# New order lists for every engine: GpSimd's wide sums laid away from VectorE's two-operand work in SBUF

## The chip, the cores and the metric

The kernel runs on one core of one Trainium2 chip. A core has five engines that run side by side, each through its own list of instructions in order: TensorE (PE in the profile, with its weight loads as PEld), VectorE (DVE), ScalarE (ACT), GpSimd (POOL) and SyncE (SP), which here only issues DMAs. They meet through semaphores: an instruction waits at the head of its engine's list until what it needs is there, and everything behind it on that engine waits with it. The metric is the time of one execution on the device, in microseconds; the runs of the kernel before took 1015.21 to 1023.01, with a median of 1018.05 over three.

## The reference, cut to what matters

There are 16 x 512 = 8192 tokens `x` of 512 float32 numbers. For every token the reference computes

```python
h = _ln(x, pw_g[pathway_ids], pw_b[pathway_ids])            # _ln: mean and variance over the 512
h = _ln(h, cp_g[compartment_ids], cp_b[compartment_ids])
t = _ln(x, tm_g[time_steps], tm_b[time_steps])              # time_steps == compartment_ids here
m, n, r = [x + _mlp_ln(state, ...)[:, None, :] for each of three conditions of the batch]
s = _ln(x, ms_g[scale_type], ms_b[scale_type])
w = softmax(aw)
cat = concatenate([w[0]*h, w[1]*t, w[2]*m, w[3]*n, w[4]*r, w[5]*s])      # 6 * 512 wide
out = x + _ln(silu(cat @ int_W1 + int_b1) @ int_W2 + int_b2, int_g, int_be)
```

There are 500 pathways, 5 compartments (and time steps) and 3 scale types by the table sizes. Everything is float32.

## The kernel before, in words

**What is multiplied.** The wide product `cat @ int_W1` is split into three products of 512 x 512 for each token: block X is `x` itself against the weighted sum of the three blocks for `m`, `n`, `r`; block H is the doubly normalised `h` against the first block; block V is the normalised `x` against one matrix that holds both `t` and `s`, `vs`, made from two blocks of `int_W1` with the gammas of the token's compartment and scale as row factors. What depends on the batch and the tables alone is a row that is gathered and added (`ga`). To have one such matrix for a whole tile, the kernel first sorts the tokens by compartment and scale (that is most of the head).

**Groups and tiles.** The sorted tokens are worked on in 16 groups ("windows") of 512, each of four tiles of 128 tokens. `build` (L337, L339 to L342; step `bd`) and `s_part` (L325, `sp`) make a new matrix where a group starts a new one. Where two tiles share a matrix and for X and H always, the 2 x 2 blocks of tokens and features are multiplied by a scheme with seven half-sized products in place of eight: `half_product` (L553, `m7`), `norm_product` (L565, `v7`), `seventh` (L672, `q7`, the second layer). Such a scheme needs sums and differences of the operands and of the results. Those of the operands are made on VectorE (`token_sum`, L508 to L516, `u1` to `u4`; `norm_sum`, L527 to L533, `yv`) or on GpSimd (`z_sums`, L658 to L664, `zs`: 128 x 256 in SBUF); those of the results on VectorE from PSUM (`half_out` L589 to L595, `r2`, `r3`, `r5`; `hidden_add` L598, `ha`; `sum_first` L689 and L691, `sf`; `sum_last` L700 and L702, `sl`) and on ScalarE (`copy_first` L580, `cf`; `keep_first`, `keep_last` L682 to L695, `kf`, `ku`). GpSimd's other wide sum is `shift_x` (L468, `sh`): it adds the last bias row to a tile of `x`, 128 x 512 in SBUF, four in each group.

**The way of a group.** GpSimd gathers the four tiles of `x` (`gx`), the rows of the pathway tables (`gh`, into two buffers), of the compartments (`gc`, two buffers) and the added rows (`ga`, four buffers), all L229. ScalarE takes the sums for mean and variance (`xs`, `fs`, L427 to L429); VectorE and GpSimd make the root of the variance (`xe`, `xp`; `fv` L445, `fp` L449); VectorE multiplies (`front_1`, L423 and L424, `f1`; `front_less`, L460, `f2`); ScalarE scales (`nv` L394, `fn` L453). VectorE then turns each tile in blocks of 32 x 32 (L255: `tx`, `tv`, `th`, `tz` for X, V, H and the hidden layer Z) into a tile `rX`, `rV`, `rH` or `rZ`, and SyncE spreads it by four DMAs of 64 KB for each quarter (`spread_row`, L263, `sX`, `sV`, `sH`, `sZ`) into `catX` to `catZ`, from which TensorE multiplies. The hidden layer goes through `ha`, a silu (`hs`, L601), `tz`, `sZ` and `q7`; then `lq` (L738), `lv` (L746) and `lp` (L751) give the last variance, `lb` (L759 and L760) normalises and adds `x`, and `po` (L764) puts the rows out by a DMA with indices, from GpSimd.

**What sets the order.** Nothing reorders: `tc.manual_schedule()` leaves each engine's instructions as the program emits them, and the program emits them by three lists of step names. `ORDER` is the head with the first two groups; `WINDOW` is run for group numbers 2 to 11, and its names hold a letter for the group (`o`, `p`, `c`, `n`, `m`: two before, one before, this, the next, the one after), so that the work on neighbouring groups interleaves; `LAST` names the rest. A name that has been run is passed over:

```python
for w in range(2, 12):
    run(WINDOW, w)
run(LAST)
```

Each engine's list is thus the subsequence of steps that it has a part in. Several tiles share a buffer and so order the work as well: `rV` and the operand sums of V (`sv`, written by `yv`) lie in one buffer, likewise `rH` with `ss` and `rZ` with `zs`; `x` has three buffers for the groups in flight, so a gather `gx` waits for the `lb` of the group three before.

Of the kernel before, what the change touches and what calls it, by code (L numbers as in the profile page):

```python
# [1716 lines left out]
```

## Time and profile before

| | before |
|---|---|
| median of three runs | 1018.05 us (1015.21 to 1023.01) |
| the profiled execution | 1015.54 us, its span 1013.5 us |
| granted TensorE clock, mean | 0.964 |
| busy share of TensorE, VectorE, ScalarE, GpSimd | 89%, 87%, 57%, 67% |

One execution of the program was taken by the profiler. A row of the timeline or of the groups gives the line of the program, the engine, the operation, what it writes and reads (out<-in), the shape, and how often; busy time is in microseconds, the mean of one instruction in nanoseconds. Idle time in front of an instruction is put down to what ended it. "Issue" is time in which the engine waited for nothing that the profile shows. The last `lv` steps (L746) of consecutive groups serve as marks for the length of a group: they start at 191.2 and at 738.3 us with ten groups between them. Ends of matmuls are modelled, and spans on GpSimd are rough.

### The profile page before, as it was taken

To read this page: it belongs to the slowest core of one execution; us is meant where nothing else is said; L and a number is where in the kernel's file an instruction comes from. 1 tells how busy PE (TensorE), PEld (TensorE's weight loads), DVE (VectorE), ACT (ScalarE), POOL (GpSimd) and SP (SyncE) were. 2 spreads that over 40 slices of the span, in tenths; PEclk is the share of its full clock that TensorE was granted. 3 is DMA by queue.
4 is the path that set the end of the run, shared out by engine and by line. 5 is a ranking of instruction groups with operands and counts; after the bars stand their busy time and mean duration, and the time that the engine had idled before them with its cause. 6 is when DMAs were issued, how large, how long until landed. Compare 5 with 4: busy or idle time off the path is not lost.

```text
span 1013.5 us, 14659 instructions
## 1 busy us (share of the span) xinstructions
PE 904.0 (89%) x3908; PEld 702.9 (69%) x3909; DVE 882.7 (87%) x1476; ACT 573.6 (57%) x1357; POOL 675.5 (67%) x735
## 2 busy tenths in 40 slices
...
GB/s 295 204 137 199 199 248 157 131 191 149 232 186 214 191 172 199 184 209 181 172 190 217 180 236 167 193 196 207 191 230 168 77 204 178 195 169 168 133 50 117
DMA packets 88513, 185.45 MB, mean 183 GB/s; under 512 B 24324, under 2 KB 24324, under 8 KB 88428
## 3 DMA queue, kind: packets, MB, share of 16 engines
...
HBM read 100.48 MB, written 19.97 MB: 119 GB/s over the span
## 4 chain that ended last, share of the span: by engine, by line
DVE 29%; PE 21%; issue 11%; SPq 8%; ACT 7%; DMA 4%; another core or an unknown queue 2%; POOL 1%; ACTq 0%; DVEq 0%; POOLq 0%
SPq L263 8%; PE u L553 6%; PE p L572 4%; PE p L553 3%; DMA catX<-rX 3%; DVE rV L255 3%; PE u L565 2%; PE pq_0b L672 2%; DVE pw L460 2%; DVE pw L423 2%; DVE sv L531 2%; DVE rX L255 2%; DVE vs L337 2%; ACT junk L738 2%
## 5 line engine op out<-in xcount | busy, mean ns | idle before, releaser
L764 POOL DMA_INDIRECT out<-yb,tok x64 | 69.7, 1089 | 67.0 <-issue 28.8
L553 PE MATMUL p<-wh__81,catH 128*128 128x256 f32 x480 | 111.4, 379 | 0.0
L553 PEld LDWEIGHTS p<-wh__81,catH 128*128 128x128 f32 x480 | 91.1, 190 | 13.0 <-issue 0.7
L229 POOL DMA_INDIRECT xbs<-in_x,tok x64 | 63.4, 990 | 48.5 <-DVE yb L760 27.6
L427 ACT ACTIVATE junk<-xbs 128x512 bf16<-128x512 f32 x64 | 40.1, 626 | 97.2 <-DMA xbs<-in_x,tok 73.4
L229 POOL DMA_INDIRECT pw<-in_pw,i_pw x64 | 64.1, 1001 | 33.7 <-issue 15.7
L229 POOL DMA_INDIRECT add<-rows,i_add x64 | 68.0, 1063 | 26.1 <-issue 12.8
L449 POOL TENSOR_TENSOR rsh<-veh,mhalf 128x1 f32<-128x1 f32 x64 | 48.2, 756 | 53.9 <-DVE veh L445 53.3
L468 POOL TENSOR_TENSOR xbs<-xbs,rows 128x512 f32<-128x512 f32 x64 | 83.5, 1309 | 0.5
L553 PE MATMUL u<-wt,catX 128*128 128x256 f32 x240 | 64.4, 417 | 21.3 <-ACT p L580 20.3
L229 POOL DMA_INDIRECT cp<-cp_rows,i_cp x64 | 67.7, 1058 | 23.1 <-issue 14.0
L601 ACT ACTIVATE add<-add 128x512 f32<-128x512 f32 x64 | 38.7, 626 | 76.6 <-DVE add L598 42.6
L565 PE MATMUL u<-vs,sv 128*128 128x256 f32 x276 | 70.1, 384 | 7.7 <-DVE sv L531 3.7
L553 PEld LDWEIGHTS u<-wt,catX 128*128 128x128 f32 x240 | 48.6, 207 | 34.3 <-ACT p L580 25.1
L424 DVE SCALAR_TENSOR_TENSOR pw<-pw,rsx 128x512 f32<-128x512 f32 x64 | 64.5, 1007 | 3.2 <-POOL rsx L377 0.9
L598 DVE TENSOR_TENSOR add<-p,add 128x512 f32<-128x512 f32 x64 | 42.2, 665 | 26.7 <-remote 19.8
L394 ACT ACTIVATE xm<-xbs,nmx,rsx 128x512 f32<-128x512 f32 x64 | 49.4, 805 | 28.1 <-DVE nmx L388 18.9
L337 DVE SCALAR_TENSOR_TENSOR vs<-wt,sct,vs 128x512 f32<-128x512 f32 x72 | 64.7, 957 | 0.4 <-ACT vs L325 0.4
L565 PEld LDWEIGHTS u<-vs,sv 128*128 128x128 f32 x276 | 50.9, 190 | 20.0 <-DVE sv L531 5.1
L427 ACT ACTIVATE junk<-pw 128x512 bf16<-128x512 f32 x60 | 37.7, 629 | 47.7 <-DVE pw L424 16.8
L453 ACT ACTIVATE pw<-pw,rsh 128x512 f32<-128x512 f32 x64 | 44.5, 714 | 34.5 <-POOL rsh L449 15.4
L759 DVE SCALAR_TENSOR_TENSOR yb<-yb,rsy,rows 128x512 f32<-128x512 f32 x60 | 57.5, 959 | 1.6 <-POOL rsy L751 1.6
...
## 6 DMA issues: line engine op xcount, KB each, us to landing
...
```

Of the source, the lines that this page charges most:

```text
L229: nc.gpsimd.indirect_dma_start(dst, None, table, bass.IndirectOffsetOnAxis(ap=idx, axis=0), **kw)
L255: nc.vector.transpose(rot[:, :, :, j, :].rearrange("p q c t -> p c q t"), src.rearrange("p (c q t) -> p c q t", c=NC, q=Q))
L263: nc.sync.dma_start(st[cat][q * L : (q + 1) * L, g].rearrange("p c t -> p (c t)"), st[rot][g * L : (g + 1) * L, q].rearrange("p c j t -> p ...
L337: nc.vector.scalar_tensor_tensor(v[:, c], wt[:, c], sct[:, c, g, w : w + 1], v[:, c], ALU.mult, ALU.add)
L394: nc.scalar.activation(t, st["xb"][:, j, :], AF.Identity, bias=st["nm"][:, j : j + 1], scale=st["rs"][:, j : j + 1])
L424: nc.vector.scalar_tensor_tensor(h, h, st["rs"][:, j : j + 1], pw[:, D:], ALU.mult, ALU.add)
L427: nc.scalar.activation(junk, x, AF.Identity, accum_out=sums[:, 0, k : k + 1])
L468: nc.gpsimd.tensor_add(st["xb"][:, j, :], st["xb"][:, j, :], rows[:, 2, :])
L553: nc.tensor.matmul(dst, m[:, c], at_["half1"][k][:, c], start=(k in (1, 1 if one_matrix(st, a) else 5) and c == 0), stop=(c == NC - 1), sk ...
L565: nc.tensor.matmul(dst, m[:, c], v_half(k)[:, c], start=(k == 5 and c == 0), stop=(c == 1), skip_group_check=True)
L759: nc.vector.scalar_tensor_tensor(y, y, st["rsy"][:, j : j + 1], rows[:, 1, :], ALU.mult, ALU.mult)
L764: nc.gpsimd.indirect_dma_start(out_rows[j], bass.IndirectOffsetOnAxis(ap=tok[:, j, w : w + 1], axis=0), yb[:, j, :], None)
```

## The change

The three lists are replaced. The steps are the same ones, with the same instructions and operands; `ORDER` holds the same 545 names, and a few names move between `WINDOW` and the lists around it because the cut between two groups lies elsewhere (for instance `u1`, `u4`, `m7.0.2` and `m7.0.6` of a group now end its own pass of `WINDOW` instead of beginning the next one). What changes is the order of each engine's instructions in the head, in the repeated groups and in the tail. GpSimd's wide sums, `zs` and `sh`, get other neighbours: in `WINDOW` for instance `sh` of tile 2 moves from the end of its own group, amid `f1`, `sf`, `sl`, to the next group behind `tz.p.1`, and `sh` of tiles 0 and 1 stand among the steps `r3`, `r5`, `ha`, whose second operand is in PSUM. Nothing in the program's functions changes.

The diff, with `WINDOW` whole and the two long lists cut to their ends:

```diff
 ORDER = """
-    lt wk.1.0 sz scl fg h2.2 lo ax g4 dk cv cg xt.0.2 xs.0.0 sp.0.0 se pwi g6 h2.1 gh.0.0 gh.0.2 he.1 fl.2 fl.0 g5 h2.0
-    bx fl.3 wm.4 by xs.0.2 dp xs.0.3 kd gt.0.0 gt.0.2 gt.1.2 gt.0.1 he.2 eh.2 cw gt.0.3 he.0 eh.1 xs.0.1 xt.0.0 xt.0.3
-    pk xe.0 xp.0 xv.0.2 xv.0.0 eh.0 cs tt cp dc gt.1.1 xm.0 nv.0.3 xt.0.1 lh tb vt.0.3 nv.0.1 vt.0.1 tk.0 gx.e0.0 f1.0.2
...
-    gc.2.2 lb.0.3 m7.1.0.5 r5.1.1 kb.1.1 gx.3.0 m7.1.1.2 u4.1.1 m7.1.0.2 u4.1.0 r2.1.0 po.0.2 th.2.1 m7.1.0.4 r2.1.1
-    ha.1.1 sp.2.0 r3.1.1 bd.2.0 th.2.0 r5.1.0 gh.2.2
+    sz h2.0 dk se h2.1 h2.2 g6 xs.0.1 he.1 xs.0.0 he.0 he.2 ax ac eh.1 xt.0.3 g4 xs.0.3 pwi xs.0.2 wk.1.2 xe.0 gh.0.0
+    scl wk.1.0 sp.0.0 g5 dp fg xt.0.0 xv.0.3 bx by kd xp.0 lt tt xm.0 nv.0.3 gh.0.2 xt.0.2 nv.0.0 xv.0.0 eh.2 dc eh.0 cs
+    cv lo fl.3 xv.0.2 gt.0.1 gt.0.2 lw wm.1 lh cg tb wh pk vt.0.3 vv.0.3 fl.2 vt.0.0 cw cp cn gt.0.0 wk.2.2 gt.1.3 ct
...
+    gx.3.0 po.0.0 sh.2.1 m7.1.1.5 m7.1.0.5 fn.2.1 xs.3.2 u4.1.0 r5.1.1 th.2.1 r3.1.1 gh.2.2 r2.1.1 sh.1.1 m7.1.0.4
+    ha.1.1 r2.1.0 po.0.2 fn.2.0 th.2.0 r5.1.0 bd.2.0
 """
...
 WINDOW = """
-    m7.p.0.2 u4.p.0 fp.c.1 fn.c.1 u1.p.1 m7.p.1.2 m7.p.0.6 u4.p.1 m7.p.1.6 lp.o lb.o.3 kb.p.0 r2.p.0 kz.m.2 po.o.3 va.n
-    lb.o.0 gx.n.0 m7.p.1.5 sp.c.0 bd.c.0 m7.p.0.5 sh.p.0 r5.p.1 gc.c.3 lb.o.2 sV.c.3 gx.n.2 xs.n.0 gx.n.3 r3.p.1
-    m7.p.0.3 m7.p.1.4 th.c.1 ha.p.0 r2.p.1 u3.c.0 ha.p.3 hs.p.3 r3.p.0 gh.c.2 th.c.0 m7.p.0.4 ha.p.1 r5.p.0 hs.p.0
-    gh.c.3 hs.p.1 lb.o.1 tz.p.3 po.o.1 m7.c.0.1 v7.c.0.1 m7.p.1.3 tz.p.0 ha.p.2 po.o.2 cf.c.0 m7.c.0.7 v7.c.0.2 hs.p.2
-    sV.c.1 yv.c.0.3 gc.c.2 v7.c.0.7 kb.p.1 xs.n.3 tz.p.1 sh.p.1 sX.c.2 gx.n.1 tz.p.2 m7.c.1.1 ga.c.3 yv.c.0.1 cf.c.1
-    f1.c.2 v7.c.0.5 yv.c.0.2 yv.c.0.4 fs.c.2 f1.c.3 v7.c.0.3 fv.c.2 v7.c.0.6 sX.c.3 u3.c.1 ga.c.1 v7.c.0.4 sp.c.2 bd.c.2
-    v7.c.1.1 sZ.p.0 q7.p.0.1 q7.p.0.2 kz.p.1 fs.c.3 po.o.0 fv.c.3 fp.c.2 cf.c.2 m7.c.1.7 yv.c.1.3 f2.c.2 f2.c.3 sZ.p.1
-    xs.n.1 sh.c.3 fn.c.2 th.c.2 sZ.p.2 fp.c.3 fn.c.3 th.c.3 zs.p.0 tx.n.1 v7.c.1.7 q7.p.0.7 zs.p.1 q7.p.0.5 zs.p.2
-    yv.c.1.1 yv.c.1.2 yv.c.1.4 kf.p.0 cf.c.3 q7.p.0.6 v7.c.1.5 v7.c.1.6 xs.n.2 vd.n gh.n.0 kf.p.1 sf.p.1 zs.p.3 q7.p.0.4
-    sf.p.0 q7.p.0.3 xe.n sZ.p.3 gh.n.1 xp.n tx.n.3 v7.c.1.3 ku.p.0 kb.p.2 sH.c.1 q7.p.1.1 q7.p.1.2 zs.p.4 tx.n.0 zs.p.5
-    sl.p.0 xm.n tx.n.2 sH.c.0 gc.n.1 sl.p.1 nv.n.3 nv.n.1 kb.p.3 q7.p.1.5 kz.p.0 q7.p.1.7 tv.n.3 tv.n.1 sH.c.2 sH.c.3
-    f1.n.0 nv.n.0 gc.n.0 nv.n.2 tv.n.2 kf.p.2 v7.c.1.2 tv.n.0 sV.n.2 kf.p.3 sf.p.3 fs.n.0 zs.p.6 q7.p.1.6 q7.p.1.4
-    ku.p.1 f1.n.1 sf.p.2 fs.n.1 sh.c.2 lq.p.1 sV.n.0 sl.p.2 f2.n.0 zs.p.7 q7.p.1.3 sl.p.3 lq.p.2 kz.c.3 ga.c.2 lq.p.3
-    fv.n.0 ga.c.0 fv.n.1 f2.n.1 u2.c.0 sX.n.1 u2.c.1 lq.p.0 u1.c.0 sX.n.0 lv.p fp.n.0 fn.n.0 v7.c.1.4
+    fp.c.1 fv.c.0 v7.p.1.2 sp.c.0 bd.c.0 r3.p.0 r2.p.0 va.n m7.p.1.2 lb.o.0 gx.n.0 gc.c.2 m7.p.1.6 u4.p.1 lb.o.3 fp.c.0
+    po.o.3 lb.o.2 sX.c.0 m7.p.1.5 r5.p.1 kb.p.1 m7.p.0.4 ha.p.1 sh.p.1 r3.p.1 m7.p.0.5 sV.c.2 fn.c.1 sX.c.2 fn.c.0
+    th.c.1 sV.c.3 u3.c.0 xs.n.0 th.c.0 gx.n.2 gh.c.2 gh.c.3 sh.p.0 r5.p.0 m7.p.1.4 ha.p.3 hs.p.1 m7.p.0.3 ha.p.0 r2.p.1
+    m7.p.1.3 hs.p.3 tz.p.3 ha.p.2 ga.c.3 kb.p.0 hs.p.0 tz.p.0 tz.p.1 m7.c.0.1 sX.c.3 sh.p.2 hs.p.2 tz.p.2 sZ.p.0
+    v7.c.0.1 cf.c.0 gx.n.3 gc.c.3 m7.c.1.1 m7.c.0.7 yv.c.0.1 xs.n.2 yv.c.0.3 v7.c.0.7 cf.c.1 po.o.0 yv.c.0.2 f1.c.2
+    v7.c.0.2 po.o.2 yv.c.0.4 v7.c.0.3 sp.c.2 ga.c.1 lb.o.1 v7.c.0.4 po.o.1 v7.c.0.5 v7.c.0.6 gx.n.1 f1.c.3 u3.c.1 bd.c.2
+    fs.c.2 fv.c.2 fp.c.2 f2.c.2 fs.c.3 kz.o.3 fv.c.3 fp.c.3 yv.c.1.3 v7.c.1.1 cf.c.2 sZ.p.1 zs.p.0 f2.c.3 fn.c.2 th.c.2
+    fn.c.3 q7.p.0.1 zs.p.1 th.c.3 zs.p.2 tx.n.1 m7.c.1.7 v7.c.1.7 kf.p.0 gh.n.0 q7.p.0.7 q7.p.0.5 tx.n.2 xs.n.3 kf.p.1
+    sf.p.1 vd.n zs.p.3 tx.n.3 sh.c.3 q7.p.0.2 xs.n.1 xe.n xp.n q7.p.0.6 gh.n.1 sf.p.0 yv.c.1.1 sZ.p.2 sZ.p.3 zs.p.4
+    zs.p.5 zs.p.6 gc.n.0 sH.c.3 ku.p.0 sl.p.0 yv.c.1.2 cf.c.3 kb.p.2 xm.n yv.c.1.4 nv.n.3 q7.p.0.3 sH.c.1 q7.p.0.4
+    sl.p.1 v7.c.1.5 v7.c.1.6 v7.c.1.3 sH.c.0 q7.p.1.2 tx.n.0 kb.p.3 nv.n.1 tv.n.3 nv.n.0 tv.n.1 q7.p.1.5 q7.p.1.1 kf.p.3
+    f1.n.0 tv.n.0 kz.p.1 q7.p.1.7 sf.p.3 kf.p.2 q7.p.1.6 kz.m.2 sH.c.2 nv.n.2 v7.c.1.4 tv.n.2 ku.p.1 sf.p.2 sl.p.2
+    f1.n.1 u2.c.0 kz.m.0 fs.n.0 u2.c.1 ga.c.2 lq.p.0 zs.p.7 q7.p.1.3 q7.p.1.4 sl.p.3 m7.c.0.2 u1.c.0 sV.n.1 u4.c.0
+    m7.c.0.6 sV.n.0 gc.n.1 fs.n.1 fv.n.1 f2.n.1 u1.c.1 lq.p.1 ga.c.0 lq.p.2 lq.p.3 lv.p lp.p sX.n.1 f2.n.0
 """
 LAST = """
-    lp.10 va.15 gc.12.2 m7.11.1.2 u4.11.1 sV.12.3 u1.11.1 sX.12.2 m7.11.0.2 fp.12.1 fn.12.1 lb.10.1 kb.11.1 gx.13.1
-    m7.11.0.6 r3.11.0 r2.11.0 m7.11.1.6 sh.11.0 r2.11.1 m7.11.1.4 lb.10.2 gx.13.2 sp.12.0 po.10.2 ha.11.3 lb.10.0
...
-    ga.15.3 sh.15.1 u4.15.1 m7.15.1.5 lq.14.0 m7.15.0.5 m7.15.0.6 r2.15.0 r3.15.0 m7.15.1.6 r2.15.1 r3.15.1 kb.14.3
-    r5.15.1 r5.15.0 hs.15.1 m7.15.0.3 m7.15.1.4 sh.15.2 ha.15.0 hs.15.0 m7.15.1.3 ha.15.3 hs.15.3 tz.15.0 q7.14.1.5
-    sh.15.3 q7.14.1.7 w2 tz.15.1 ha.15.2 tz.15.3 hs.15.2 tz.15.2 kf.14.3 sf.14.3 q7.14.1.1 kf.14.2 q7.14.1.6 ku.14.1
-    zs.14.7 q7.14.1.4 q7.14.1.3 sl.14.2 sh.14.0 sl.14.3 q7.14.1.2 lq.14.3 sZ.15.0 sf.14.2 lq.14.2 lv.14 lp.14 lb.14.0
-    po.14.0 lb.14.1 po.14.1 lb.14.3 po.14.3 lb.14.2 l2.15.0 la.15.0 yg.15.0 lq.15.0 sZ.15.1 l2.15.1 po.14.2 la.15.1
-    yg.15.1 lq.15.1 sd.15.1 rv.15.1 ft.15.1 po.15.1 sd.15.0 rv.15.0 sZ.15.2 l2.15.2 la.15.2 yg.15.2 ft.15.0 po.15.0
-    lq.15.2 sZ.15.3 sd.15.2 rv.15.2 ft.15.2 l2.15.3 la.15.3 yg.15.3 lq.15.3 sd.15.3 rv.15.3 po.15.2 ft.15.3 po.15.3
+    va.13 kb.11.0 sV.12.3 kb.11.2 r3.11.0 fp.12.1 fn.12.1 gc.12.3 fv.12.0 fp.12.0 fn.12.0 m7.11.1.6 r2.11.1 sX.12.0
+    r3.11.1 r2.11.0 sX.12.2 lb.10.3 gx.13.3 v7.11.1.2 sV.12.2 xs.13.3 lb.10.2 gx.13.2 m7.11.0.4 m7.11.1.2 xs.13.2
...
+    cf.15.3 bd.15.3 sH.15.2 lW.15.3 m7.15.1.2 ga.15.3 sH.15.3 m7.15.1.4 u2.15.1 u2.15.0 u1.15.0 m7.15.0.5 m7.15.0.6
+    u4.15.0 ku.14.1 sl.14.2 sl.14.3 u4.15.1 u1.15.1 m7.15.1.5 lq.14.1 e1 lq.14.3 lq.14.0 sf.14.2 ga.15.2 lq.14.2 lv.14
+    ga.15.0 m7.15.1.6 r5.15.0 r2.15.0 r3.15.0 lp.14 lb.14.3 po.14.3 ha.15.3 r5.15.1 r3.15.1 hs.15.3 m7.15.0.3 ha.15.0
+    hs.15.0 r2.15.1 tz.15.3 m7.15.1.3 ha.15.2 hs.15.2 tz.15.0 m7.15.0.4 ha.15.1 hs.15.1 sh.14.1 tz.15.2 tz.15.1 sZ.15.0
+    sh.14.2 lb.14.2 lb.14.0 w2 po.14.0 po.14.2 sh.15.1 lb.14.1 po.14.1 sh.15.2 l2.15.0 la.15.0 yg.15.0 lq.15.0 sh.15.3
+    sZ.15.2 l2.15.2 la.15.2 lq.15.2 yg.15.2 sd.15.0 rv.15.0 ft.15.0 po.15.0 sd.15.2 sZ.15.1 l2.15.1 la.15.1 yg.15.1
+    rv.15.2 sZ.15.3 ft.15.2 po.15.2 lq.15.1 sd.15.1 rv.15.1 ft.15.1 l2.15.3 la.15.3 lq.15.3 po.15.1 yg.15.3 sd.15.3
+    rv.15.3 ft.15.3 po.15.3
 """
```

More of the change, by code (lines that the diff above doesn't have):

```diff
@@ new lines @@
+    nv.0.2 nv.0.1 wk.1.3 gc.0.2 xt.0.1 xv.0.1 do va.0 ca gt.0.3 cm cr f1.0.0 gc.0.0 tk.0 wk.1.1 vt.0.1 gx.e0.0 vv.0.0
+    gx.e0.3 vv.0.1 vt.0.2 wk.2.0 gx.e0.2 vv.0.2 f1.0.2 gt.1.1 rp.1 rc.1 ro.1 gx.e0.1 wk.2.1 rp.0 rc.0 wk.2.3 lX.0.0
+    fs.0.0 xs.e0.0 xs.e0.3 gt.1.0 lX.0.1 fs.0.2 f2.0.0 fv.0.0 fp.0.0 fl.0 xs.e0.1 fv.0.2 fp.0.2 f2.0.2 vd.0 bd.0.0
+    gr.e0.0 fn.0.2 ht.0.2 gr.e0.1 xs.e0.2 xe.e0 rp1 gh.0.1 xa.0 xp.e0 xm.e0 ro.0 lX.0.2 fn.0.0 ht.0.0 wm.3 gt.1.2 tk.1
+    gx.e1.0 gx.e1.1 gx.e1.3 xs.e1.1 ea.0 nv.e0.0 gx.1.0 gh.0.3 fl.1 mt.e0.0 nv.e0.1 mt.e0.1 rp2 ar ey.0 ez.0 f1.0.1
@@ L54 @@
+    lq.0.0 lq.0.1 lq.0.3 lq.0.2 lv.0 u1.1.1 sX.2.2 nv.2.0 tv.2.0 r3.1.0 nv.2.2 tv.2.2 sV.2.1 fs.2.0 sV.2.2 fv.2.0 gc.2.2
+    lp.0 sh.1.0 sV.2.3 fp.2.0 lb.0.2 gx.3.2 m7.1.0.2 kb.1.0 lb.0.3 lb.0.0 kb.1.1 sp.2.0 m7.1.1.2 u4.1.1 f2.2.0 sV.2.0
+    gx.3.0 po.0.0 sh.2.1 m7.1.1.5 m7.1.0.5 fn.2.1 xs.3.2 u4.1.0 r5.1.1 th.2.1 r3.1.1 gh.2.2 r2.1.1 sh.1.1 m7.1.0.4
+    ha.1.1 r2.1.0 po.0.2 fn.2.0 th.2.0 r5.1.0 bd.2.0
 """
 WINDOW = """
[L58 removed]
@@ new lines @@
+    q7.11.1.7 sf.11.3 lq.11.0 fs.13.1 fv.13.1 ga.12.0 sV.13.2 q7.11.1.6 ku.11.1 kb.12.0 u2.12.0 u1.12.0 sX.13.0
+    q7.11.1.4 gc.13.0 u2.12.1 fs.13.0 fp.13.1 f2.13.1 fn.13.1 q7.11.1.3 sl.11.2 sl.11.3 m7.12.0.5 lq.11.2 ga.12.3
+    lq.11.3 sp.13.1 fv.13.0 u1.12.1 m7.12.0.2 r5.12.0 sX.13.2 m7.12.0.6 va.14 lv.11 u4.12.1 m7.12.1.5 m7.12.1.6 u4.12.0
+    fp.13.0 f2.13.0 fn.13.0 lp.11 lb.11.3 gx.14.3 lb.11.2 xs.14.3 r3.12.0 th.13.1 r3.12.1 r2.12.0 th.13.0 lb.11.0
+    r2.12.1 m7.12.0.4 ha.12.1 hs.12.1 m7.12.1.3 ha.12.2 r5.12.1 hs.12.2 m7.12.0.3 ha.12.0 hs.12.0 po.11.2 tz.12.2
```

144 lines of the change are left out of this document (66 added, 78 removed).

## The prediction

> **What bounds the kernel now.** I read the page first, for its time and each engine's share.
>
> ```profile
> span 1013.5 us, 14659 instructions
> PE 904.0 (89%) x3908; PEld 702.9 (69%) x3909; DVE 882.7 (87%) x1476; ACT 573.6 (57%) x1357; POOL 675.5 (67%) x735
> ```
>
> Two engines are nearly full: TensorE (PE) and VectorE (DVE). A share over the whole span says nothing of a stage, so the second view is the table of stretches: head, first group, ten groups of the steady loop together, two groups alone, tail, end.
>
> ```profile
> 0.00:130.00 130.00, 108.68 (x568) 64.69 (x569) 88.16 (x220) 76.22 (x192) 95.63 (x167) 0.95 0.64 208
> 130.00:191.20 61.20, 51.29 (x196) 37.45 (x196) 47.13 (x66) 30.67 (x76) 38.15 (x37) 0.94 0.61 176
> 191.20:738.30 547.10, 503.90 (x2240) 424.00 (x2239) 514.60 (x824) 314.67 (x758) 378.75 (x377) 0.98 0.67 193
> 356.30:413.70 57.40, 51.06 (x226) 43.35 (x225) 55.07 (x87) 33.05 (x80) 38.31 (x38) 0.97 0.64 184
> 413.70:467.00 53.30, 49.63 (x225) 42.02 (x225) 50.45 (x79) 30.55 (x75) 38.41 (x38) 1.00 0.68 198
> 738.30:990.80 252.50, 227.77 (x881) 171.59 (x880) 218.58 (x342) 146.78 (x321) 152.77 (x146) 0.95 0.55 156
> 990.80:1013.50 22.70, 12.36 (x29) 5.13 (x27) 14.21 (x25) 5.24 (x13) 10.23 (x9) 0.82 0.36 119
> ```
>
> The columns are length, then busy time (and count) of PE, PEld, DVE, ACT, POOL. The ten steady groups take 547.1 us, 54.7 each. A plain group (413.7 to 467.0) takes 53.3, with PE busy 49.6 and VectorE 50.5. A group that also rebuilds the products' matrix (356.3 to 413.7; eight more VectorE instructions) takes 57.4, with VectorE busy 55.1. So VectorE looks like the fuller engine. But is all of that work? The third view, the timeline, says no:
>
> ```profile
> 452.04 0.71 POOL L658 TENSOR_TENSOR zs<-catZ 128x256 f32<-128x256 f32 x1
> 452.05 0.98 DVE L700 TENSOR_TENSOR yb<-yb 128x256 f32<-128x256 f32 x1
> 456.08 1.24 POOL L662 TENSOR_TENSOR zs<-catZ 128x256 f32<-128x256 f32 x1
> 456.78 2.33 DVE L424 SCALAR_TENSOR_TENSOR pw<-pw,rsx 128x512 f32<-128x512 f32 x1
> 457.30 1.26 POOL L468 TENSOR_TENSOR xbs<-xbs,rows 128x512 f32<-128x512 f32 x1
> 458.52 1.17 POOL L664 TENSOR_TENSOR zs<-catZ,zs 128x256 f32<-128x256 f32 x1
> 459.03 1.29 DVE L255 STREAM_TRANSPOSE rV<-xm 128x512 f32<-128x512 f32 x2
> 461.33 0.75 DVE L424 SCALAR_TENSOR_TENSOR pw<-pw,rsx 128x512 f32<-128x512 f32 x1
> 472.97 2.46 DVE L759 SCALAR_TENSOR_TENSOR yb<-yb,rsy,rows 128x512 f32<-128x512 f32 x1
> 473.58 1.29 POOL L468 TENSOR_TENSOR xbs<-xbs,rows 128x512 f32<-128x512 f32 x1
> 486.57 2.19 DVE L527 TENSOR_TENSOR sv<-catV 128x256 f32<-128x256 f32 x1
> 487.18 1.28 POOL L468 TENSOR_TENSOR xbs<-xbs,rows 128x512 f32<-128x512 f32 x1
> ```
>
> Columns: start, duration. The same L424 takes 0.75 when GpSimd (POOL) does no wide sum and 2.33 beside two of them; two transposes (L255) beside a wide sum keep their 0.65 each. An operation with its second operand in PSUM is not slowed either:
>
> ```profile
> 148.91 1.28 POOL L468 TENSOR_TENSOR xbs<-xbs,rows 128x512 f32<-128x512 f32 x1
> 149.02 0.69 DVE L598 TENSOR_TENSOR add<-p,add 128x512 f32<-128x512 f32 x1 [6.26 <-issue]
> ```
>
> What this costs in a plain group, by the groups of 413.7 to 467.0 against the free durations:
>
> ```profile
> L759 DVE SCALAR_TENSOR_TENSOR yb<-yb,rsy,rows 128x512 f32<-128x512 f32 x4 | 4.7, 1171 | 0.0
> L424 DVE SCALAR_TENSOR_TENSOR pw<-pw,rsx 128x512 f32<-128x512 f32 x4 | 4.6, 1146 | 0.1
> L460 DVE SCALAR_TENSOR_TENSOR pw<-pw,sumsh,cp 128x512 f32<-128x512 f32 x4 | 3.8, 977 | 0.0
> L527 DVE TENSOR_TENSOR sv<-catV 128x256 f32<-128x256 f32 x2 | 3.1, 1536 | 0.0
> L531 DVE TENSOR_TENSOR sv<-catV 128x256 f32<-128x256 f32 x2 | 2.7, 1372 | 0.0
> ```
>
> ```profile
> L531 DVE TENSOR_TENSOR sv<-catV x23: 402/416/3105, 155.5 to 758.7; 128x256 f32<-128x256 f32 x23
> ```
>
> With 0.75 free for the three wide lines and 0.42 (the median above) for the two narrow ones: L759 4.7 − 3.0 = 1.7, L424 4.6 − 3.0 = 1.6, L460 0.8, L527 3.1 − 0.84 = 2.3, L531 1.9. Together 8.3 us. The four `sh` sums (L468) carry most of it, 1.6 to 1.8 each; a `zs` sum costs some 0.5 (L700, 0.98 where 0.42 is free: 0.56). Without them VectorE would do 42 us of work in a group of 53.3, and PE would be the bound.
>
> What PE loses is in the waits of a plain group and of one that rebuilds:
>
> ```profile
> PE pq_1b L672 <- DVE yb L691: 1.2, 1, 1.2
> PE p L565 <- DVE sv L533: 1.0, 1, 1.0
> PE u L565 <- DVE sv L527: 0.5, 1, 0.5
> ```
>
> ```profile
> PE u L553 <- ACT p L580: 4.5, 1, 4.5
> ```
>
> In the plain group 2.7 of its 3.7 us of PE idle time end at a VectorE instruction queued behind one that a wide sum had held. In the rebuilding group 4.5 of 6.3 end at `cf` (L580), the copy that lets a second product be added on.
>
> **The change part by part.** Instructions and data stay; only lists move. The first term is the wide sums' place. I read it from the new WINDOW by what stands before each sum in GpSimd's list, since that is what holds it at run time. `sh.p.1` stands behind `po.o.3`, which waits for `lb.o.3`; the put-out costs about 1 us, in which VectorE does `lb.o.2`; then come `r5`, `ha`, `r3`, all with an operand in PSUM: free. `sh.p.0` stands behind `gh.c.2` (it reuses a buffer that `th.c.0` frees) and `gh.c.3`; after `th.c.0` VectorE has `r5`, `ha`, `ha`, `r2` and transposes: free. `sh.p.2` stands behind `ga.c.3`, whose buffer `tz.p.3` frees; `ha.p.2` and three transposes follow, some 2.7 us by the rows above (0.69 + 3 × 0.65), against 1 us of gather and 1.28 of sum: just free. `sh.c.3` follows `zs.p.3` behind `gh.n.0`, beside transposes and `sf`: free if GpSimd is not late. Of the eight `zs`, numbers 1, 2 and 3 lie beside transposes and `sf`; 0, 4, 5, 6, 7 still meet `f2`, `sl`, `yv` or `u`. In the old list the next two VectorE steps behind each of the four `sh` hold four steps with such an operand pair; in the new one they hold one (the `yv` behind `sh.p.2`). So 3 × 1.75 = 5.2 of 8.3 go: 0.6 of the contention.
>
> What that is worth in time is bounded by PE. Plain groups: six, with at most 53.3 − 49.6 = 3.7 to win; of the 2.7 that waits name I take 0.6, 1.6, rounded to 1.5: 6 × 1.5 = 9. Rebuilding groups: four, the first of the ten among them, which waits alike:
>
> ```profile
> PE u L553 <- ACT p L580: 5.4, 1, 5.4
> ```
>
> The old ACT list has three silus ahead of `cf.c.0`, the new one four, so `cf` now waits for `ha.p.2`. From `bd.c.0` to `ha.p.2` VectorE has 31 instructions in the new list, at about 0.65 some 20 us, and PE has 19 us of products ahead of the one that needs `cf`: ten `m7` (eight `m7.p`, `m7.c.0.1`, `m7.c.1.1`) by 1.73 and two `v7` by half of that. The 1.73 is half the step between two runs of sixteen matmuls, two products each:
>
> ```profile
> 251.58 3.62 PE L553 MATMUL u<-wt,ss 128*128 128x256 f32 x16
> 255.03 3.62 PE L553 MATMUL u<-wx__80,ss 128*128 128x256 f32 x16
> ```
>
> Counted in the same way the old lists have about 20 against 20, and yet PE waited 4.5, because VectorE came into the group late by what contention had cost it in the group before. With 5.2 less it comes in early: of 4.5 I take 3.0, 4 × 3.0 = 12. Below: nothing gained, 0. Above: all PE idle time of the steady stretch, 547.1 − 503.9 = 43.
>
> Head (0 to 191.2): only reordered, with hardly a wide sum before 130. PE idles 21.3 + 9.9 there. Moves in both directions; bounds ±6, value 0. Tail (738.3 to 990.8): by the same reading 16 `sh` meetings become 12, 4 × 1.75 = 7 us of VectorE time, at the steady rate (21 us of time for 52 of contention) 3 us. End (22.7): all `q7` now precede the last `m7`; that uncovers the last `ha`, `tz` and spread (before, seven `q7` of 0.87 lay over them) and takes `lb.14` out of the end: 0, ±4.
>
> Other queues: the gathers `gx`, `gh`, `gc`, `ga` and the put-outs `po` change places on GpSimd, which is busy 38.4 of 53.3; ACT, which waits for their landings, has 30.6 of 53.3. Those slacks hide them; if they fail, ACT's `cf` is late, as now. `kz` does nothing after the first group. The weight loads keep SP's order but for table loads in the head.
>
> Sum: −9 − 12 − 3 = −24. Profiled execution 1015.5 (span 1013.5 and 2.0 around it) becomes 991.5; the median of the runs, 1018.05, lies 2.5 above it, so 994.
>
> [...]
>
> **The rivals.** (1) The sums run away from their places: forecast no change. For it: in the old list `zs.p.6` stands behind `sf.p.3`, and it ran at 456.08, before `f1.n.1`'s L424 at 461.33 by five microseconds, in the midst of the earlier L424. If the new places drift alike, other operand pairs are met, contention stays at 8.3 and the time with it: 1016. Against: three of four `sh` now stand right behind a step that waits for VectorE.
>
> (2) PE becomes the full bound: plain groups fall to about 50.5, rebuilding ones to 52, 547 to 511; −36 there and −4 in the tail: 978. For it: VectorE would have eight microseconds to spare. Against: latencies of the spreads are not shortened.
>
> (3) Slower: the spreads through SP. The first `yv` writes a tile in the buffer that `rV` holds, so it must wait for the last `sV` spread.
>
> ```profile
> 407.09 4.97 SPq L263 DMA_DIRECT2D catV<-rV  x8
> 417.22 6.27 SPq L263 DMA_DIRECT2D catV<-rV  x8
> 431.74 0.41 DVE L531 TENSOR_TENSOR sv<-catV 128x256 f32<-128x256 f32 x1
> ```
>
> A spread is four issues, 4.97 / 2 = 2.5 us. The last `sV` was sixth of a run of eight spreads, issued by 423.5, and the first `yv` ran at 431.7: 8.2 later, of which some 3 are landing. Now the last `sV` is seventh: 2.5 later, and VectorE arrives 5 earlier. Behind `yv` queue `f1`, `bd`, `f2` and all that PE's `v7` needs. It decides from the point where the last `sV` lands over 8 us after VectorE is free for it; if that holds PE 4 us a group, ten groups give +40, less the 24: 1034.
>
> **How the numbers follow.** Forecast 0.50, its own range 983 to 1007; rival 2 0.16; rival 1 0.22; rival 3 0.12. The likeliest is 994. For 8 in 10 the range takes rival 1 whole and most of rival 2: 975 to 1024. About 1% (1008 to 1028) is what a measurement of this kernel can tell from no change. Forecast and rival 2 lie below: faster 0.66; rival 1: same 0.22; rival 3: slower 0.12.
>
> **What would show it.** Right: L527, L531, L424, L759 near their free means in the steady groups, VectorE busy about 45 in a plain one, `pq_1b <- yb L691` and `u <- p L580` smaller, groups of some 52 and 54. Wrong: those groups as long as before with VectorE idle instead (rival 3, with a wait for catV or catX in front of L527 or L531), or the same excess at other lines (rival 1).

## The result and the profile after

Four runs of the changed kernel took 981.35 to 988.67 us, with a median of 983.36; the kernel before took 1015.21 to 1023.01 beside them, with a median of 1017.68. The ratio is 0.966, with a 95% interval of 0.961 to 0.972: 34 us faster, where 24 were forecast. The profiled execution of after is the slowest of its four runs (988.67). The same kernel was therefore profiled once more on another chip (called "after again" here): 979.70 against 1018.42 us, a ratio of 0.963 (0.959 to 0.968), its profiled execution 976.82. Lines in after are one higher than in before, since the lists are one line longer; in the experiments they are up to four higher.

The head of the page of after, and its stretches cut at the same marks as before (the last `lv`, now L747): head, ten steady groups, tail with end, and one plain group. Columns as in the prediction.

```profile
span 986.8 us, 14570 instructions
PE 902.2 (91%) x3908; PEld 707.5 (72%) x3909; DVE 787.2 (80%) x1476; ACT 578.6 (59%) x1357; POOL 670.5 (68%) x735
```

```profile
0.00:190.80 190.80, 162.66 (x752) 103.14 (x754) 125.83 (x283) 105.02 (x261) 133.24 (x201) 0.92 0.63 196
190.80:730.00 539.20, 504.89 (x2251) 430.84 (x2250) 450.77 (x827) 321.69 (x764) 373.06 (x377) 0.98 0.68 196
730.00:986.80 256.80, 234.70 (x908) 173.51 (x906) 210.57 (x368) 151.87 (x335) 164.22 (x157) 0.97 0.57 164
...
514.00:567.50 53.50, 50.54 (x226) 43.50 (x225) 43.00 (x80) 30.93 (x74) 37.12 (x38) 0.97 0.68 197
```

The steady groups and the tail of after again, and one of its plain groups:

```profile
194.80:722.20 527.40, 499.68 (x2252) 427.25 (x2251) 450.94 (x828) 322.16 (x764) 371.71 (x377) 0.99 0.70 201
722.20:975.00 252.80, 233.00 (x908) 172.82 (x906) 208.82 (x367) 151.73 (x334) 164.39 (x157) 0.97 0.58 167
...
409.00:460.40 51.40, 48.83 (x226) 42.33 (x225) 42.98 (x79) 31.04 (x74) 37.12 (x38) 1.00 0.71 205
```

VectorE's work in the steady groups falls from 514.6 to 451 us in both, with the same instructions. What that is worth differs between the two executions: 547.1 us of steady groups become 539.2 in one and 527.4 in the other. The tail with its end was 275.2 (252.5 and 22.7 in the prediction's rows) and is 256.8 and 252.8. The head was 191.2 and is 190.8 and 194.8.

The groups of VectorE's instructions in that plain group of after (514.0 to 567.5), with the lines that the prediction named:

```profile
L425 DVE SCALAR_TENSOR_TENSOR pw<-pw,rsx 128x512 f32<-128x512 f32 x4 | 3.0, 752 | 0.1
L760 DVE SCALAR_TENSOR_TENSOR yb<-yb,rsy,rows 128x512 f32<-128x512 f32 x4 | 3.0, 745 | 0.0
...
L256 DVE STREAM_TRANSPOSE rH<-pw 128x512 f32<-128x512 f32 x4 | 2.7, 701 | 3.9 <-ACT pw L454 3.9
...
L528 DVE TENSOR_TENSOR sv<-catV 128x256 f32<-128x256 f32 x2 | 2.1, 1030 | 0.0
...
L532 DVE TENSOR_TENSOR sv<-catV 128x256 f32<-128x256 f32 x2 | 0.8, 413 | 0.0
```

L425, L760 and L532 are free (they meant 1146, 1171 and 1372 before). L528 is the one pair that the prediction left: one `yv` a group still meets `sh.p.2`. Against the free durations a plain group has 2.2 us of excess over all of VectorE's lines, where the same count gives 9.7 before. So the contention went as planned. The new row is 3.9 us in front of `th` (L256): VectorE now waits for ScalarE, whose own wait stands one step earlier, at the copy `cf.c.2` (below). Where TensorE waits in the steady groups, before, in after and then in after again:

```profile
PE u L553 <- ACT p L580: 15.4, 7, 5.4
PE pq_1b L672 <- DVE yb L691: 12.1, 10, 1.2
PE p L565 <- DVE sv L533: 6.3, 6, 1.1
```

```profile
PE u L554 <- ACT p L581: 22.5, 10, 3.5
PE p L566 <- ACT p L581: 3.6, 1, 3.6
PE u L554 <- issue: 2.8, 1, 2.8
```

```profile
PE u L554 <- ACT p L581: 16.8, 8, 2.7
PE p L566 <- ACT p L581: 3.3, 1, 3.3
```

Of the waits for `sv` and for `yb` (L691 before) that the prediction named, 1.7 us are left in after and 1.9 in after again, of 22.9 (the rows above and two smaller ones). The wait for `cf` did not become smaller, which the prediction had named as a sign of being right: 15.4 us before, 22.5 and 16.8 now. And it sits elsewhere: in front of the second product of a rebuilding group at most 1.3 us of it are left, but it stands in front of `m7.c.1.7` in most groups, behind `cf.c.2`. That place in after, by time (start, duration):

```profile
534.23 1.53 POOL L765 DMA_INDIRECT out<-yb,tok  x1 [0.30 <-issue]
...
538.73 1.03 PE L566 MATMUL u<-vs,catV 128*128 128x256 f32 x4
538.82 0.97 POOL L765 DMA_INDIRECT out<-yb,tok  x1 [0.30 <-issue]
539.60 1.03 PE L673 MATMUL pq_0a<-w,catZ 128*128 128x256 f32 x4
540.10 0.98 POOL L230 DMA_INDIRECT xbs<-in_x,tok  x1 [0.30 <-issue]
541.11 1.09 POOL L450 TENSOR_TENSOR rsh<-veh,mhalf 128x1 f32<-128x1 f32 x2
...
542.82 0.57 ACT L581 COPY p<-u 128x512 f32<-128x512 f32 x1 [3.79 <-remote]
...
543.44 3.67 PE L554 MATMUL u<-wt,catX 128*128 128x256 f32 x8 [2.82 <-ACT p L581]
```

`cf.c.2` (the copy at 542.82) needs the product of 538.73, which by its row is done at 539.8. It starts 3 us later; no row says why ("remote"). ScalarE has the scalings `fn` behind this copy and VectorE `th` behind them; GpSimd's part of them (L450) was done at 542.2, before the copy began. What stands beside the copy is a run of seven gathers and put-outs on GpSimd without a break (531.6 to 541.1). The eight matmuls behind the wait take 3.67 us. Elsewhere eight of this form take 1.95 to 2.0: after the pause TensorE ran them at half its clock (the granted clock is 0.50 from 543.6 to 547.0 us). There are six such spells in the steady groups of after, three in after again and three before (granted clock over all of those groups 0.98, 0.99 and 0.98).

### The profile page after: what moved, and what is told of

It is laid out like the page before. It is cut to its first block, busy times and chain, and to the rows that moved or that the text cites. A ratio compares the mean times of both kernels' runs of the same rounds, so it can differ in the third digit from the quotient of the medians.

```text
span 986.8 us, 14570 instructions
## 1 busy us (share of the span) xinstructions
PE 902.2 (91%) x3908; PEld 707.5 (72%) x3909; DVE 787.2 (80%) x1476; ACT 578.6 (59%) x1357; POOL 670.5 (68%) x735
## 5 line engine op out<-in xcount | busy, mean ns | idle before, releaser
L230 POOL DMA_INDIRECT xbs<-in_x,tok x64 | 70.3, 1098 | 42.3 <-DVE yb L761 27.4
L554 PE MATMUL u<-wt,catX 128*128 128x256 f32 x240 | 62.1, 405 | 25.6 <-ACT p L581 22.5
L581 ACT COPY p<-u 128x512 f32<-128x512 f32 x60 | 34.4, 575 | 85.4 <-remote 40.7
L566 PE MATMUL u<-vs,sv 128*128 128x256 f32 x276 | 75.1, 412 | 8.2 <-ACT p L581 5.6
L230 POOL DMA_INDIRECT cp<-cp_rows,i_cp x64 | 66.7, 1042 | 22.9 <-issue 14.4
L450 POOL TENSOR_TENSOR rsh<-veh,mhalf 128x1 f32<-128x1 f32 x64 | 51.5, 810 | 32.2 <-DVE veh L446 22.4
L566 PEld LDWEIGHTS u<-vs,sv 128*128 128x128 f32 x276 | 55.9, 207 | 22.4 <-ACT p L581 11.0
L752 POOL TENSOR_TENSOR rsy<-vey,mhalf 128x4 f32<-128x4 f32 x15 | 20.8, 1387 | 67.6 <-DVE vey L747 67.6
L256 DVE STREAM_TRANSPOSE rH<-pw 128x512 f32<-128x512 f32 x60 | 41.4, 702 | 31.0 <-ACT pw L454 30.8
L554 PE MATMUL u<-wx__80,catX 128*128 128x256 f32 x240 | 57.5, 384 | 0.8 <-DVE add L599 0.8
L554 PE MATMUL u<-wx__80,ss 128*128 128x256 f32 x240 | 56.6, 380 | 0.5 <-DVE add L590 0.5
L554 PE MATMUL p<-wt,catH 128*128 128x256 f32 x240 | 56.5, 379 | 0.0
```

Source lines behind the costliest of these rows:

```text
L230: nc.gpsimd.indirect_dma_start(dst, None, table, bass.IndirectOffsetOnAxis(ap=idx, axis=0), **kw)
L256: nc.vector.transpose(rot[:, :, :, j, :].rearrange("p q c t -> p c q t"), src.rearrange("p (c q t) -> p c q t", c=NC, q=Q))
L450: nc.gpsimd.tensor_tensor(rs, st.pop(("ve", j)), mhalf[:, :1], ALU.pow)
L554: nc.tensor.matmul(dst, m[:, c], at_["half1"][k][:, c], start=(k in (1, 1 if one_matrix(st, a) else 5) and c == 0), stop=(c == NC - 1), sk ...
L566: nc.tensor.matmul(dst, m[:, c], v_half(k)[:, c], start=(k == 5 and c == 0), stop=(c == 1), skip_group_check=True)
```

## Experiments: one part alone

Each with the kernel before on the same chip; ratios are to it (1017.31 us here).

```diff
 e1_head:    ORDER of after;            WINDOW, LAST of before
 e1_groups:  WINDOW of after;           ORDER, LAST of before
+  LAST = "fv.12.0 fp.12.0 fn.12.0 sX.12.0 v7.11.1.2 sV.12.2 sh.11.2" + LAST
 e1_tail:    LAST of after;             ORDER, WINDOW of before
+  LAST = "lp.10 m7.11.0.2 u1.11.1 u4.11.0 m7.11.0.6 sV.12.1" + LAST
```

> The lists of before with the new ORDER alone. The prediction's step and the trace (first marks at 191.2 and 190.8): 0 us, so about 1018, within 6.

Measured: 1016.15 us, 0.998 (0.996 to 1.001). The head gives nothing.

> The lists of before with the new WINDOW alone (seven names that it leaves undone stand ahead of the old LAST). The prediction's step: 21 us, so about 997. The trace of after says that the ten steady groups give 8 us: about 1010. In both, VectorE's excess over its free durations falls from 9.7 to 2.2 us in a steady group.

Measured: 996.42 us, 0.978 (0.975 to 0.982): 20.9 us, the forecast's 21. The execution that was profiled took 1008.08 and is not in the ratio; by the marks it lost its time in head and tail. Its steady groups:

```profile
193.40:721.20 527.80, 500.34 (x2244) 426.44 (x2243) 449.14 (x824) 319.26 (x756) 369.11 (x375) 0.99 0.69 200
```

That is 19.3 us less than before's 547.1, as in after again; the 7.9 of the first profile of after are the exception.

> The lists of before with the new LAST alone (six names that the old WINDOW leaves undone stand ahead of it). The prediction's step: the tail gives 3 us, so about 1015. Theory S (GpSimd's back-to-back gathers and put-outs hold TensorE's completion signals back; the old tail has runs of eight to eleven of them, the new one has not): 15 to 18 us, so about 1001.

Measured: 999.54 us, 0.982 (0.978 to 0.986): 17.8 us, six times the forecast's 3. The tail with its end, and TensorE's waits in before's tail:

```profile
741.40:997.60 256.20, 234.80 (x911) 173.25 (x909) 210.00 (x367) 151.44 (x334) 161.92 (x155) 0.97 0.57 164
```

```profile
PE p L572 <- ACT p L580: 6.2, 1, 6.2
...
PE u L553 <- ACT p L580: 4.9, 1, 4.9
PE u L565 <- issue: 4.3, 1, 4.3
```

Of the 19.0 us between 275.2 and 256.2, TensorE's busy time gives 5.3 (240.1 to 234.8; half-clock spells that are gone: the granted clock there is 0.97, and was 0.94) and its idle time 13.7. Three of the old waits, 6.2, 4.9 and 4.3, begin in GpSimd's runs of nine, eight and eleven gathers and put-outs. Of these 15.3 us one wait of 2.7 is left; against that stands a new wait at the end of the program, for the last spread of `rZ` (in after: `PE p L614 <- DMA catV<-rZ: 6.2, 1, 6.2`). The three parts sum to 39.8; together they gave 34.3 in the first comparison and 38.7 in the second.

## Experiments: the run of seven

```diff
 GpSimd's names of WINDOW, in order (e1_split)
- ga.c.3 sh.p.2 gx.n.3 gc.c.3 po.o.0 po.o.2 ga.c.1 po.o.1 gx.n.1 fp.c.2 fp.c.3 zs.p.0 zs.p.1 zs.p.2 gh.n.0 zs.p.3 sh.c.3
+ ga.c.3 gx.n.3 sh.p.2 gc.c.3 po.o.0 po.o.2 po.o.1 fp.c.2 fp.c.3 zs.p.0 zs.p.1 zs.p.2 gx.n.1 gh.n.0 zs.p.3 ga.c.1 sh.c.3
```

In this kernel tile 1 of `x` is transposed ahead of its gather, so the transposed tile holds the `x` of an earlier group; the work is the same, but VectorE does not wait there.

> After, with three names of WINDOW moved, so that GpSimd's run of seven gathers and put-outs ahead of fp.c.2 becomes a run of four (gx.n.3 goes ahead of sh.p.2, gx.n.1 behind zs.p.2, ga.c.1 ahead of sh.c.3). Theory S: cf.c.2 starts within 1 us of its product, TensorE's wait in front of m7.c.1.7 falls from 2.8 us to under 1 and the spells at half the clock behind it go; 2 to 4 us in each of nine groups, so about 955 to 965. Rival Q (TensorE stands because only one product of the second layer lies between v7.c.1.1 and m7.c.1.7, whatever GpSimd does): the wait stays and the time is that of after, about 983, within 4.

Measured: 980.86 us, 0.966 (0.961 to 0.971). Rival Q is out: the wait in front of `m7.c.1.7` is gone from the plain groups, and of six half-clock spells one is left (mean granted clock 0.979, where after has 0.966). But the time hardly moved, since `gx.n.1` now lands late, `xs.n.1` waits for it on ScalarE, and `cf.c.3` queues behind: 1.7 to 2.4 us of TensorE in front of `v7.c.1.5`. The corrected version exchanges tiles 0 and 1 in their transposes and takes three names ahead of the late one:

```diff
 e3_split: as e1_split, and in WINDOW
-  tx.n.1 (behind zs.p.2) ... tx.n.0 (behind q7.p.1.2) ...  xs.n.1 xe.n xp.n q7.p.0.6 gh.n.1 sf.p.0 yv.c.1.1 ... yv.c.1.2 cf.c.3
+  tx.n.0                 ... tx.n.1                   ...  sf.p.0 yv.c.1.1 cf.c.3 xs.n.1 xe.n xp.n q7.p.0.6 gh.n.1 ... yv.c.1.2
```

> After, with the run of seven gathers broken to four and the order put right: tiles 0 and 1 of x exchanged in their transposes (so that VectorE does not stand in front of the late one), sf.p.0, yv.c.1.1 and cf.c.3 ahead of xs.n.1 and xe.n. On a chip that holds signals back: 15 to 25 us below after. On one that doesn't: within 5 us of after.

Measured, beside after again: 972.04 us, 0.954 (0.950 to 0.958), against its 979.70, 0.963 (0.959 to 0.968). It is the fastest version that does the whole work on the chips where before takes about 1018, 7.7 us below after instead of the 15 to 25 expected. In the profiled executions the steady groups give 3.2 of it (524.2 for 527.4); the rest shows in no profile. The same place in it:

```profile
536.57 1.09 PE L567 MATMUL u<-vs,catV 128*128 128x256 f32 x4
536.79 1.00 POOL L451 TENSOR_TENSOR rsh<-veh,mhalf 128x1 f32<-128x1 f32 x1 [0.16 <-issue]
537.49 1.03 PE L674 MATMUL pq_0a<-w,catZ 128*128 128x256 f32 x4
537.69 0.57 ACT L582 COPY p<-u 128x512 f32<-128x512 f32 x1
...
538.36 1.95 PE L555 MATMUL u<-wt,catX 128*128 128x256 f32 x8
```

Same products, same copy: now it starts at the modelled end of its product, TensorE does not stop, and the eight matmuls take 1.95 us. No half-clock spell is left in its steady groups (granted clock 1.00). What is late next, in its steady groups, is `sf.p.0`:

```profile
PE pq_0a L674 <- DVE yb L691: 9.6, 8, 1.2
```

An earlier try (`e2_split`) differs from `e3_split` in one thing: it exchanged tiles 1 and 2, so that the late tile was turned as the second of the four.

> After, with GpSimd's run of seven gathers and put-outs broken to four as in the run before, and what then came late put right: tx.n.1 and tx.n.2 exchanged (tile 1 of x is gathered later), and sf.p.0, yv.c.1.1 and cf.c.3 ahead of xs.n.1 and xe.n, so that they don't wait for that gather. Theory S (the run held TensorE's completion signals back): the wait in front of m7.c.1.7 stays away, the new one in front of v7.c.1.5 (2.0 to 2.4 us) goes as well, plain groups of 49 to 50 us instead of 53.4: about 955 to 970. Rival B (TensorE is bound elsewhere by then): another wait of 2 us a group appears and the time stays at about 980.

Measured, on a chip where before takes 993.44: 999.19 us, 1.005 (1.002 to 1.007). VectorE stood in front of the late tile with `sf.p.1` and `sf.p.0` behind it, and TensorE waited up to 5.1 us in every group:

```profile
PE pq_0a L674 <- DVE yb L691: 38.5, 10, 5.1
```

So the gain of a list can be lost by one transposition that waits; rival B's other wait appeared, and it was made by the experiment.

## Experiments: what the sums cost, and their place alone

The chip of the next two, as of `e2_split`, is another one: before takes 993.44 us on it.

```diff
 def shift_x(st, j):
-    nc.gpsimd.tensor_add(st["xb"][:, j, :], st["xb"][:, j, :], rows[:, 2, :])
+    nc.gpsimd.memset(st["xb"][:, j, :], 0.0)          # in before: e2_free_before; in after: e2_free_after
```

> Before, with the sum of shift_x replaced by a write of zeros to the same tile: the last bias row and x in the result are left out; waits and lists stay, and GpSimd reads nothing in SBUF there. It prices what the four sums of a group cost in the old lists. The prediction's step (a sum of four is worth as much as the three it priced at 21 us in the groups and 3 in the tail): 30 us or more, about 985. Rival V (VectorE's time is slack, and the gain came from somewhere else): under 8 us, about 1012.

> The same in the lists of after. If their sums lie apart from VectorE's two-operand work, as the trace shows (2.2 us of excess in a group), little is left to win: 0 to 6 us, about 980.

Measured: 939.74 us, 0.945 (0.942 to 0.948), with the lists of before, and 943.05, 0.948 (0.945 to 0.951), with those of after. The steady groups and a plain group of the first, then the steady groups of the second:

```profile
184.60:689.80 505.20, 494.85 (x2245) 425.52 (x2244) 455.46 (x824) 312.08 (x757) 347.96 (x377) 0.99 0.73 209
...
389.70:438.60 48.90, 48.85 (x225) 42.34 (x224) 43.44 (x80) 30.18 (x75) 34.71 (x38) 1.00 0.77 216
```

```profile
193.00:694.70 501.70, 492.25 (x2252) 424.17 (x2251) 437.97 (x827) 321.83 (x764) 344.28 (x377) 1.00 0.73 211
```

With sums that read nothing, and on a chip where TensorE's wait at the run of nine is 0.95 us and not 6.18 (rows in the next section), the old lists are as good as the new ones: a plain group takes 48.9 us with TensorE busy for 48.85. So there, with GpSimd's work lighter, the old order of the other engines holds nothing up. The same is true of the tail: with its end it takes 248.1 us in the old lists (689.8 to 937.9) and 249.5 in the new ones (694.7 to 944.2), though the old runs of eleven, eight and nine stand in it. The 54 us are no pure price of contention, since a write takes GpSimd 0.53 us on average instead of 1.31. And this write does not slow VectorE: L759 keeps 0.75 beside it in `e2_free_before`, where beside a sum it took 2.46 before.

```profile
395.64 0.75 DVE L759 SCALAR_TENSOR_TENSOR yb<-yb,rsy,rows 128x512 f32<-128x512 f32 x1
396.23 0.57 POOL L468 MEMSET xbs<- 128x512 f32 x1
```

The other half of the question is whether moving the sums does it without the rest. Four names of before's WINDOW are moved:

```diff
 GpSimd's names of WINDOW, in order (e3_sums)
- gx.n.0 sh.p.0 gc.c.3 gx.n.2 gx.n.3 gh.c.2 gh.c.3 po.o.1 po.o.2 gc.c.2 sh.p.1 gx.n.1 ga.c.3 ga.c.1 po.o.0 fp.c.2 sh.c.3 fp.c.3
+ gx.n.0 gc.c.3 sh.p.0 gx.n.2 gx.n.3 gh.c.2 sh.p.1 gh.c.3 po.o.1 po.o.2 gc.c.2 gx.n.1 ga.c.3 ga.c.1 po.o.0 fp.c.2 fp.c.3
- zs.p.0 zs.p.1 zs.p.2 gh.n.0 zs.p.3 gh.n.1 xp.n zs.p.4 zs.p.5 gc.n.1 gc.n.0 zs.p.6 sh.c.2 zs.p.7
+ zs.p.0 zs.p.1 zs.p.2 gh.n.0 zs.p.3 gh.n.1 sh.c.3 xp.n zs.p.4 zs.p.5 gc.n.1 gc.n.0 zs.p.6 zs.p.7 sh.c.2
```

> Before, with the four sums of a group alone moved to other places in GpSimd's list of WINDOW, beside transposes and operations with an operand in PSUM; nothing else changes, head and tail neither. Theory C (the contention of these sums is what the new order of the groups removes): VectorE's excess in a group falls from 9.7 to 3 us or less, and the steady groups win 30 to 42 us of the 42 that they won where the sums read nothing. Rival O (the other engines' orders carry the gain): under 10 us.

Measured: 1007.84 us, 0.990 (0.985 to 0.994): 10.6 us, just above what rival O allowed. Its steady groups, and one of TensorE's waits in them:

```profile
190.20:728.40 538.20, 504.33 (x2241) 427.69 (x2240) 473.41 (x824) 312.05 (x758) 384.46 (x377) 0.97 0.68 196
```

```profile
PE u L566 <- ACT p L581: 5.6, 1, 5.6
```

VectorE's excess fell only to 4.7 us a group, since the `zs` kept their places and the moved sums still meet some pairs. A plain group falls by about 1.6 us (51.0 for 52.6, one with the wait above aside) for 5 us of excess taken away, the rate that the forecast had used (1.5 for 5.2). But the moved sums had stood between gathers: without them GpSimd has runs of seven and eight in each group and once one of eleven, and the 5.6 us above stand behind that one. So the contention is a cause: in the plain groups the move gives all that the new WINDOW gives (51.0, and 51.5 in after again). Over the whole it is worth half of it; the other half lies in that wait and in the rebuilding groups, which fall from 57.8 us to 56.4 with the sums alone and to 54.6 in after again.

```diff
 e3_sums_tail: WINDOW of e3_sums, ORDER of before, LAST of e1_tail
```

> The moved sums of the run before together with the new LAST. Theory C and the trace of the tail: the gains of the groups and of the tail add up: on a chip that holds signals back about 18 us below the moved sums alone, on one that doesn't 0 to 5 us; in both as fast as after or faster.

Measured: 987.37 us, 0.971 (0.966 to 0.975): 20.5 us below the moved sums alone, so the parts add up; it stays above after.

## Experiments: runs of gathers, and two kinds of chip

After itself was run again beside these:

> After, unchanged, on the chip of these runs. Two chips have shown themselves: on one, TensorE's completion signals come 2 us late while GpSimd issues a long run of gathers, and before takes 1017 us; on the other they come in 0.4 us whatever GpSimd does, and before takes 993. Theory: on a chip that holds signals back, the ratio to before is 0.966 as measured. On one that doesn't, the groups win more (the wait in front of m7.c.1.7 is not there: plain groups of about 49.5 us instead of 53.3, 35 to 40 us in all) and the tail wins less (0 to 5 us): 0.955 to 0.965, about 955.

Measured: 0.963, as told above. On this chip before takes 1018.42, and the updates of TensorE's semaphore are recorded late beside runs of gathers, as in after (table in the last section); on the chip where before takes 993.44 after was not timed.

To test the tail, names of GpSimd's list are moved there (ten, not the eleven of the expectation):

```diff
 e2_tailruns, LAST of before
- gx.13.2 po.10.2 gx.13.0 gx.13.3 po.10.1 gh.12.2 gh.12.3 gc.12.3 po.10.0 po.10.3 ga.12.3 sh.11.1 ga.12.0
+ gx.13.2 po.10.2 gx.13.0 gx.13.3 sh.11.1 gh.12.2 gh.12.3 gc.12.3 ga.12.3 ga.12.0 po.10.1 po.10.0 po.10.3
   (and po.11.0 po.11.2 po.11.3 behind gx.14.1; po.12.1 po.12.3 po.12.0 behind gx.15.2)
```

> Before, with eleven of GpSimd's names moved in LAST alone (put-outs po behind the wait of the next gather, one sum into the first run), so that its runs of eleven, eight and nine back-to-back gathers and put-outs in the tail become shorter; no other engine's list changes. Theory S: the stalls of 4.3, 4.9 and 6.2 us on TensorE there and the half-clock spells behind them go or shrink to a third: 10 to 16 us, about 1003. Rival O (the tail's gain came from the other engines' orders): about 1017, within 4.

Measured: 1001.98 us against 993.44, 1.009 (1.006 to 1.011): slower. It fell on the chip where before takes 993.44. There the run of nine has hardly a stall beside it (0.95 us, in the rows of `e2_free_before` below), so this run could not show the gain; it shows a price: put-outs that come later hold `zs`, and with it TensorE:

```profile
PE pq_0b L674 <- POOL yb L660: 3.4, 1, 3.4
```

How the chips differ on which before takes 1018 and 993 is best seen where the same list meets the same run of nine. First before, on the chip of the first profile:

```profile
871.54 1.89 PE L553 MATMUL p<-wh__81,catH 128*128 128x256 f32 x8
...
878.01 0.97 POOL L229 DMA_INDIRECT cp<-cp_rows,i_cp  x1 [0.31 <-issue]
879.93 0.69 DVE L598 TENSOR_TENSOR add<-p,add 128x512 f32<-128x512 f32 x1 [6.44 <-remote]
883.07 1.22 PE L572 MATMUL p<-vs,catV 128*128 128x512 f32 x1 [6.18 <-ACT p L580]
```

Then `e2_free_before`, with the lists of before, on the other chip:

```profile
805.44 1.89 PE L553 MATMUL p<-wh__81,catH 128*128 128x256 f32 x8
...
807.37 0.69 DVE L598 TENSOR_TENSOR add<-p,add 128x512 f32<-128x512 f32 x1
...
811.73 2.84 PE L572 MATMUL p<-vs,catV 128*128 128x512 f32 x6 [0.95 <-ACT p L580]
```

The `ha` (L598) reads the product of the first row. Here it starts 0.04 us after the product's modelled end; there 6.5 us after, 0.95 behind the end of the run.

## Why the prediction came out right, and where it did not

**Contention.** The step said that three of four sums find free places and 0.6 of the excess goes. Shown: 9.7 to 2.2 us in a plain group, more than the 5.2 of 8.3 that were forecast (VectorE is busy 43.0 in such a group, not 45), and the sum that was left is the one that the step named (`yv` behind `sh.p.2`). Rival 1, sums that run away from their places, did not happen.

**Groups: 21 us.** Right in size. In after again plain groups take 49.7 to 53.1 us, 51.5 on average for 52.6 before (forecast 52), and rebuilding ones 54.6 for 57.8 (forecast 54): 7.0 us in the six and 12.7 in the four make 19.7, where 9 and 12 were forecast. The new WINDOW alone gave 20.9. The step on `cf` in a rebuilding group, 3.0 of 4.5 us, came out at 3.2 in two of the four; the row is from after again:

```profile
375.18 1.99 PE L554 MATMUL u<-wt,catX 128*128 128x256 f32 x8 [1.27 <-ACT p L581]
```

In the first of the four the wait of 5.4 went and one of 3.3 for the next copy came. The third (467.0 to 523.6) had no such wait over 1 us before, which the prediction passed over; it won 3.4 us all the same, since three waits of 1.1 to 1.7 us for VectorE went. So the size of the term is in part luck.

The step that failed here is a cover. The prediction let ScalarE's and GpSimd's slack hide the moved gathers, and said that if they fail `cf` is late. They failed: seven in a row stand beside `cf.c.2`, and TensorE waits 0.7 to 3.5 us for it in most groups, in some with a half-clock spell of 3.4 us behind, which costs 1.7. The 12 us between the two profiles of after lie here: 28.9 us of waits for `cf` against 20.1 by the rows above, and six spells against three. With the run broken the groups come to 524.2 us (`e3_split`), and rival 2's plain groups of 50.5 are there, not its 511.

**Head: 0.** Right. **End: 0.** The end can't be compared by its mark, since `lv.14` stands earlier in the new LAST; the uncovered spread that the term named is there, as the wait of 6.2 us told above, so it is not 0, and the tail pays for it.

**Tail: 3 us.** This term was mis-sized: 17.8 alone, 18.4 in the first traces. It counted 16 sums against 12 by the steady rate. It passed over the waits of 4 to 6 us on TensorE that were in the trace of before and that end in a releaser given as "remote" or "issue", and it did not ask what stood beside them: runs of eight to eleven gathers and put-outs. The new LAST has none longer than seven. That those runs are the cause is argued: for one stall of 6.2 us the pair of rows above shows the same run with it and without it, on two chips and with other sums, but no run took the runs alone out of the tail on a chip where before takes about 1018. The sums' part of it was not measured by itself either.

**What one sum costs.** In the prediction's three rows of a slowed instruction beside an L468 sum, it starts 0.5 to 0.6 us ahead of the sum's row and ends 0.3 to 0.6 behind it; spans on GpSimd are rough. By these rows L527 takes 2.19 us where 0.42 is free, 1.77 more beside a sum of 1.28. Beside GpSimd's write, which reads nothing, L759 takes 0.75 us, beside a sum 2.46. What it is in a sum that slows VectorE no run shows.

**Rival 3** (spreads hold the first `yv`) did not come: VectorE waits for a spread once in ten groups, 1.7 us. The result lies on the forecast's side and, with 983, at the edge of its own range of 983 to 1007, since the tail gave more. In the first profile, where the groups gave 7.9 and not 21, the total came near the forecast only because the tail gave 18.4 and not 3: that sum is luck.
